# Diagonal weight matrices of a depthwise convolution built on VectorE and ScalarE instead of GpSimd

## The chip, the cores and the metric

The kernel runs on one core of a Trainium2 chip. A core has a matrix engine (TensorE, PE in the profile), VectorE (DVE), ScalarE (ACT), GpSimd (POOL) and a queue engine that issues the transfers (SyncE, SP). Each works through its own list of instructions in order, and they meet only at semaphores. The metric is the time of one execution on the device in microseconds (us); a figure for a kernel is the median of its runs.

## The reference, cut to what matters

The network has four layers on an input of 4 images of 64 x 64 positions and 96 channels. Layers 0 and 1 are state-space scans over the image in four directions, layer 2 is linear attention with a quantized feed-forward part, layer 3 a Fourier mixer with another. All is in fp32 at the interfaces. The change lies in the feed-forward part (FFN) of layer 1:

```python
def msffn(y, in_w, in_b, dw1, dw3, dw5, ln_g, ln_b, out_w, out_b):
    hcl = jax.nn.silu(y @ in_w.T + in_b)             # 192 -> 768 channels
    hc = hcl.transpose(0, 3, 1, 2)
    hc = hc + dwconv(hc, dw1) + dwconv(hc, dw3) + dwconv(hc, dw5)
    hn = layernorm(hc.transpose(0, 2, 3, 1), ln_g, ln_b)
    return hn @ out_w.T + out_b
```

`dwconv` is a depthwise convolution: each of the 768 channels has its own 1x1, 3x3 and 5x5 filter. Since all three are linear and the input is added too, they are one 5x5 filter of 25 taps for each channel.

## The kernel before, in words

`net` runs four stages one after the other: the scans of layers 0 and 1, `layer1_ffn`, `layer2` and `layer3`. Within `layer1_ffn` an image is cut into two strips of 32 rows, so there are 8 strips (n = 0 to 7), and the 768 channels into 6 tiles of 128 (t = 0 to 5). Tensors have channels on the partitions.

Once, at the start, the function loads its weights and folds the 3x3 and 1x1 filters into `taps`, a 128 x 6 x 25 tensor (lines 1244 and 1246, on VectorE). Four of the six tiles are convolved on PE (`ON_PE = (0, 2, 3, 5)`). PE can multiply by one tap for each channel if the taps stand on the diagonal of a matrix, so `diag` holds, for each of those tiles and each of the 25 taps, four 32 x 32 diagonal blocks, one for each group of 32 partitions: `eye` (the identity, stacked four times) times the tap of each partition. That makes 100 instructions of 128 x 32, on GpSimd in the kernel before (line 1249). The other two tiles (1 and 4) are convolved on VectorE, tap by tap, straight from `taps` (lines 1363 and 1365).

Then, for each strip and tile:

- `enter`: GpSimd clears a padded buffer of 36 x 68 positions (line 1289), tag `padp` with two buffers for the PE tiles and `padv` with one for the VectorE tiles. PE multiplies by the input weights in pieces of 512 positions into the PSUM tag `c` with two buffers (line 1298), and ACT applies Silu and writes the piece into the padded buffer (line 1306). A third `padp` can be cleared only when PE has finished with the first.
- `on_pe`: 25 taps times 16 small matmuls of 32 x 32 by 512 into four PSUM banks `d0` to `d3` (line 1329); then ACT copies them to `hcp` (line 1344), 16 copies for a tile.
- `on_dve`: one multiplication and 24 multiply-and-add steps over 128 x 2048 into `hcv`.
- `leave`: PE sums each finished tile over the channels into the mean (`s`, line 1375); when all six are there, the mean is subtracted (line 1410, VectorE), the squares are summed, and the strip is normalized, multiplied by the output weights (line 1455), added to the residual and stored.

The order of the instructions in each engine's list is fixed when the kernel is built. In this stage it is written by a small planner, `Plan`: each generator (`loads`, `leave`, `enter` twice, `on_pe`, `on_dve`) announces an engine and an expected time before it issues its instructions, and the planner takes the one that could start first, the earlier added one on a tie. What is issued before the planner runs, the folding of the taps and the making of the diagonals among it, announces nothing. It is ordered by the framework's own scheduler, together with the end of the stage before. In the resulting list of GpSimd stand three clearings (padp, padv, padp), then the 100 diagonals, then the clearing for the third PE tile.

Of the kernel before, what the change touches and what calls it, by code (L numbers as in the profile page):

```python
# [15 lines left out]
AF = mybir.ActivationFunctionType  # L16
# [1189 lines left out]
def layer1_ffn(k, a, x_in, y_in, x_out):  # L1206

    nc = k.nc
# [3 lines left out]
    with ExitStack() as ctx:  # L1212
# [23 lines left out]
        ON_PE = (0, 2, 3, 5)  # L1236
        taps = k.load(w, a["L1_dw5"], "taps")
        dw3 = k.load(w, a["L1_dw3"], "dw3")
        dw1 = k.load(w, a["L1_dw1"], "dw1")
        diag = k.t(w, [128, len(ON_PE), 25, 32], "diag")  # L1240
        eye = k.load(w, a["eye_blocks"], "eye")
        for t in range(NT):
            inner = taps[:, t, :].rearrange("p (y x) -> p y x", x=5)[:, 1:4, 1:4]
            nc.vector.tensor_add(inner, inner, dw3[:, t, :].rearrange("p (y x) -> p y x", x=3))
            mid = taps[:, t, 12:13]
            nc.vector.scalar_tensor_tensor(mid, mid, 1.0, dw1[:, t, :], op0=ALU.add, op1=ALU.add)
            if t in ON_PE:
                for tap in range(25):
                    nc.gpsimd.tensor_scalar_mul(diag[:, ON_PE.index(t), tap, :], eye, taps[:, t, tap : tap + 1])


        cb = k.t(w, [C, 1], "cb")
# [703 lines left out]
def net(tc, a, out):  # L1956
    with ExitStack() as ctx:
        k = Kit(tc, ctx.enter_context(tc.tile_pool(name="const", bufs=1)))
        dram = ctx.enter_context(tc.tile_pool(name="dram", bufs=1, space=DRAM))
        x1 = k.t(dram, [C, B, L], "x1")  # L1960
        x2 = k.t(dram, [C, B, L], "x2")
        x3 = k.t(dram, [C, B, L], "x3")
        y1 = k.t(dram, [DI, B, L], "y1")
        scan_layers(k, a, a["x"], x1, y1)
        layer1_ffn(k, a, x1, y1, x2)
        layer2(k, a, x2, x3)
        layer3(k, a, x3, out)
# [143 lines left out]
```

## Time and profile before

| | us |
|---|---|
| median of 3 runs | 15879.18 |
| lowest and highest run | 15832.05 and 15962.23 |
| profiled execution | 15861.73 |
| its span, first to last instruction | 15859.9 |
| the FFN of layer 1 within it | about 12750 to 14700 |

| engine | busy us | share of the span |
|---|---|---|
| PE (matmul) | 13616.6 | 86% |
| DVE | 12867.0 | 81% |
| ACT | 8291.1 | 52% |
| POOL | 9781.6 | 62% |

The shares are averages over stages that are very different. Of POOL's busy time 7186.7 us are one multiplication in the scans (line 928), and of the FFN only the start uses POOL heavily. Times in the timelines count from the span's start. In a row of groups, the figures after the shape are busy time, mean duration in ns, and the idle time of the engine just ahead of these instructions with what ended most of it. A wait in brackets names the instruction that released the waiting one.

### The profile page before, as it was taken

What the parts mean: (1) busy time and instruction counts of PE and PEld (TensorE: products, weight loads), DVE (VectorE), ACT (ScalarE), POOL (GpSimd) and SP (SyncE); (2) the same over time, 40 slices, a digit from 0 to 9 for tenths busy, and PEclk for the clock granted to TensorE, in tenths of its full rate; (3) what the DMA queues carried; (4) which work ended last, traced back from release to release, by engine and by line L of the source; (5) the groups of instructions that cost most, each with busy time, mean ns of one, the idle gap of its engine ahead of it and who ended that gap; (6) DMA issues with size and microseconds to landing.
All of it is one profiled execution on the core that took longest, in us unless ns stands there. A gap on an engine that the chain in (4) does not pass through costs nothing. (4 is left out here: it accounts for less than half of the span.)

```text
span 15859.9 us, 190275 instructions
## 1 busy us (share of the span) xinstructions
PE 13616.6 (86%) x70721; PEld 4897.8 (31%) x70721; DVE 12867.0 (81%) x9642; ACT 8291.1 (52%) x14188; POOL 9781.6 (62%) x4913
## 2 busy tenths in 40 slices
PE   7888888888888888888888888888888889998877
PEld 3222322232223222322222223222222234443344
DVE  1989798979897989799979997999899965665555
ACT  3656465556565655556655655656556522332333
POOL 0788688867886788677757775777677730000223
PEclk8888888888898888888888888888888899998888
DMA  2333433343334333433343334333433310000132
GB/s 71 110 103 121 153 108 104 120 152 106 104 122 153 106 103 120 154 109 115 113 150 118 108 118 147 111 122 116 141 118 108 115 53 18 18 11 14 46 75 70
DMA packets 662747, 1637.10 MB, mean 103 GB/s; under 512 B 102822, under 2 KB 268459, under 8 KB 658044
## 3 DMA queue, kind: packets, MB, share of 16 engines
q1 hardware_dynamic: 624956, 1549.37, 30.9%
q0 software_dynamic: 36864, 75.55, 1.6%
q8 instruction: 560, 9.18, 0.2%
q14 instruction: 367, 3.01, 0.1%
HBM read 1295.03 MB, written 329.58 MB: 102 GB/s over the span
## 5 line engine op out<-in xcount | busy, mean ns | idle before, releaser
L928 POOL TENSOR_TENSOR hc<-h,bc 128x1024 f32<-128x1024 f32 x3072 | 7186.7, 2359 | 2360.7 <-DVE h L918 1949.8
L918 DVE TENSOR_TENSOR_SCAN h<-da,state,t 128x1024 f32<-128x1024 f32 x2304 | 5271.5, 2329 | 11.5 <-ACT da L906 8.7
L939 PE MATMUL y<-hc,gather_y 128*32 128x512 f32 x12288 | 4270.8, 687 | 628.4 <-POOL hc L928 465.1
L911 DVE TENSOR_TENSOR t<-u,bc 128x1024 f32<-128x1024 f32 x3072 | 3601.2, 1218 | 895.2 <-PE u L898 780.8
L906 ACT ACTIVATE da<-dts,L_A_logs 128x1024 f32<-128x1024 f32 x3072 | 3488.0, 1147 | 726.7 <-DMA dts<-dt_dram 444.4
L898 PE MATMUL u<-dtu,spread 32*128 32x512 f32 x3072 | 1879.7, 739 | 369.4 <-DVE t L911 362.9
L962 PE MATMUL y<-L_diag,zeros 96*32 96x256 f32 x5218 | 1736.9, 463 | 0.0
L918 DVE TENSOR_TENSOR_SCAN h<-da,t 128x1024 f32<-128x1024 f32 x768 | 1711.0, 2269 | 13.1 <-ACT da L906 12.5
L939 PEld LDWEIGHTS y<-hc,gather_y 128*32 128x32 f32 x12288 | 800.1, 117 | 2404.0 <-issue 1210.4
L830 PE MATMUL m<-xs,proj 96*128 96x512 f32 (+1 forms) x2048 | 1018.3, 620 | 121.8 <-ACT dt L839 62.7
L867 ACT COPY dt<-m 96x512 f32<-96x512 f32 x512 | 297.1, 580 | 1458.9 <-PE m L862 1458.9
L898 PEld LDWEIGHTS u<-dtu,spread 32*128 32x128 f32 x3072 | 595.1, 214 | 1433.1 <-issue 1117.5
L962 PEld LDWEIGHTS y<-L_diag,zeros 96*32 96x32 f32 x5218 | 617.2, 132 | 1274.9 <-issue 1114.7
L1289 POOL MEMSET padp<- 128x2448 f32 x32 | 68.6, 2143 | 1396.7 <-PE d L1329 1375.5
L1365 DVE SCALAR_TENSOR_TENSOR hcv<-padv,taps,hcv 128x2048 f32<-128x2048 f32 x384 | 902.2, 2350 | 13.4
L1329 PE MATMUL d<-padp,diag 32*32 32x512 f32 x25600 | 885.5, 601 | 2.0 <-ACT hcp L1344 2.0
L822 POOL TENSOR_TENSOR dtu<-sp_z,dtu 96x1024 f32<-96x1024 f32 x256 | 604.4, 2361 | 384.7 <-ACT dtu L820 382.3
L862 PE MATMUL m<-sp_z,ident 96*96 96x512 f32 x1024 | 537.1, 606 | 195.6 <-ACT sp_z L856 195.6
L834 ACT ACTIVATE sp_z<-m,L_dtb 96x512 f32<-96x512 f32 x512 | 349.3, 682 | 540.4 <-PE m L830 531.6
L1329 PEld LDWEIGHTS d<-padp,diag 32*32 32x32 f32 x25600 | 483.4, 103 | 370.6 <-issue 197.7
L986 ACT COPY spare<-m 128x512 f32<-128x512 f32 x384 | 225.6, 587 | 711.0 <-PE m L983 710.8
L830 PEld LDWEIGHTS m<-xs,proj 96*128 96x128 f32 (+1 forms) x2048 | 322.4, 177 | 829.4 <-issue 325.8
(275 smaller groups left out, 15623.6 us busy)
## 6 DMA issues: line engine op xcount, KB each, us to landing
bc<-bc_dram SPq DMA_DIRECT2D x1024, 512.0 KB
dts<-dt_dram SPq DMA_DIRECT2D x768, 512.0 KB
dt_dram<-dt SPq DMA_DIRECT2D x256, 384.0 KB
y_tok<-spare SPq DMA_DIRECT2D x64, 768.0 KB
dt<-y_tok SPq DMA_DIRECT2D x128, 384.0 KB
x_tok<-y_rows SPq DMA_DIRECT2D x32, 768.0 KB
z_t<-z_rows SPq DMA_DIRECT2D x64, 384.0 KB
dx<-x_tok SPq DMA_DIRECT2D x64, 384.0 KB
```

Of the source, the lines that this page charges most:

```text
L822: rest = lambda half: nc.gpsimd.tensor_add(r[:, half], z[:, half], r[:, half])
L830: nc.tensor.matmul(ps, proj[:, src, to], xs[:, src, cols], start=src == 0, stop=src == 1)
L862: nc.tensor.matmul(ps, k.ident[:C, :C], term[:, half, cols], start=at == 0, stop=at == 2)
L898: self.nc.tensor.matmul(seg.u[:, cols], self.spread[rows, :], seg.dtu[rows, half, cols], start=True, stop=True)
L906: self.nc.scalar.activation(da, seg.dts[cb], AF.Exp, scale=seg.bt.lay.neg_a[:, seg.kd, g : g + 1])
L911: self.nc.vector.tensor_mul(gr.t, gr.seg.u, self.bc[:, 0, gr.sg, :])
L918: self.nc.vector.tensor_tensor_scan(gr.h[:, order], gr.da[:, order], gr.t[:, order], start, op0=ALU.mult, op1=ALU.add)
L928: self.nc.gpsimd.tensor_mul(gr.hc, gr.h, self.bc[:, 1, gr.sg, :])
L939: nc.tensor.matmul(seg.y[at : at + GC, :], self.gather_y, gr.hc[:, part * CH : (part + 1) * CH], start=gr.sg == 0, stop=gr.sg == NSG - 1, ...
L962: self.nc.tensor.matmul(gr.seg.y[at : at + GC, :256], self.zeros, gr.seg.bt.lay.diag.rearrange("p h t c -> p (h t c)")[:, :256], start=Fal ...
L1329: nc.tensor.matmul(pc[i][j * 32 : (j + 1) * 32, :], diag[mine, ON_PE.index(t), tap, :], pad[mine, j * 8 + dy : j * 8 + dy + 8, dx : dx + H ...
L1365: nc.vector.scalar_tensor_tensor(to, win, wt, to, op0=ALU.mult, op1=ALU.add)
```

## The change

The 100 diagonals are no longer made by GpSimd. Those of the first two PE tiles (t = 0 and 2) are made by VectorE, with the same operation; those of the other two (t = 3 and 5) by ScalarE, as an activation with the identity function and the tap as its scale, one for each partition. The values and the tensor are the same.

```diff
-            if t in ON_PE:
-                for tap in range(25):
-                    nc.gpsimd.tensor_scalar_mul(diag[:, ON_PE.index(t), tap, :], eye, taps[:, t, tap : tap + 1])
+            for tap in range(25 if t in ON_PE else 0):
+                to, one = diag[:, ON_PE.index(t), tap, :], taps[:, t, tap : tap + 1]
+
+                if t in ON_PE[:2]:
+                    nc.vector.tensor_scalar_mul(to, eye, one)
+                else:
+                    nc.scalar.activation(to, eye, AF.Identity, scale=one)
```

In the lists of the built kernel, VectorE has 50 instructions more, between the folding of the taps and its first convolution step; ScalarE has 50 more, between the last activation of the scans (line 655) and the loading of the table for Silu; GpSimd has 100 fewer, so that the clearing for the third PE tile follows the first three directly. The lists of PE and of the transfer queue are as before.

## The prediction

> **What bounds the kernel now.** I read the page first, for the stage; then the table of stretches and the waits inside that stage; then the timeline engine by engine around the operation that moves. The change touches one short place: the start of the FFN of layer 1, at 12.76 ms of a span of 15.86 ms.
>
> The page gives the chain that ended last by engine, and three groups of the stage:
>
> ```profile
> PE 12%; DVE 2%; DMA 1%; ACT 1%; issue 0%; POOL 0%; SPq 0%; ACTq 0%; POOLq 0%; DVEq 0%
> L1289 POOL MEMSET padp<- 128x2448 f32 x32 | 68.6, 2143 | 1396.7 <-PE d L1329 1375.5
> L1365 DVE SCALAR_TENSOR_TENSOR hcv<-padv,taps,hcv 128x2048 f32<-128x2048 f32 x384 | 902.2, 2350 | 13.4
> L1329 PE MATMUL d<-padp,diag 32*32 32x512 f32 x25600 | 885.5, 601 | 2.0 <-ACT hcp L1344 2.0
> ```
>
> The shares add up to some 17% of the span, because the chain is followed back only to 13.05 ms. Over that part it is PE's, so a microsecond that PE wins or loses early in the FFN should reach the end. The next view is the table of stretches (length, then busy time of PE, PE's weight loads, DVE, ACT and POOL with counts, then clock and DMA):
>
> ```profile
> 12762.90:12787.40 24.50, 18.66 (x102) 8.27 (x104) 2.72 (x16) 7.06 (x10) 24.50 (x71) 0.80 0.57 132
> 12787.40:12846.60 59.20, 37.99 (x783) 18.43 (x766) 56.45 (x25) 8.01 (x14) 59.20 (x30) 0.84 0.01 2
> ```
>
> POOL is busy for all of both, but runs 71 instructions in 24.5 us and only 30 in the next 59.2. In the second stretch PE is busy for just 38 of 59. The timelines of POOL, ACT and PE say why (start, duration, engine, line; in brackets the idle time ahead and its releaser):
>
> ```profile
> 12762.89 83.78 POOL L1249 TENSOR_SCALAR diag<-eye,taps 128x32 f32<-128x32 f32 x100
> 12846.60 2.14 POOL L1289 MEMSET padp<- 128x2448 f32 x1
> ...
> 12820.69 2.35 ACT L1344 COPY hcp<-d 32x512 f32<-32x512 f32 x4 [4.41 <-PE d L1329]
> 12823.06 0.37 ACT L1306 ACTIVATE padp<-c,in_b 128x128 f32<-128x128 f32 x1
> 12823.45 2.35 ACT L1344 COPY hcp<-d 32x512 f32<-32x512 f32 x4
> 12848.77 0.69 ACT L1306 ACTIVATE padp<-c,in_b 128x512 f32<-128x512 f32 x1 [22.98 <-POOL padp L1289]
> ...
> 12820.98 4.49 PE L1298 MATMUL c<-y,in_w 96*128 96x128 f32 x12
> 12853.16 3.72 PE L1375 MATMUL s<-hcp,avg 128*32 128x512 f32 x8 [27.70 <-ACT hcp L1344]
> ```
>
> The 100 diagonals hold POOL until 12846.6. Behind them waits the clearing of the third padp buffer; ACT stands 22.98 us for that buffer, with the evacuations of the first tile (hcp) queued behind; PE then stands 27.70 us for hcp. One chain of three waits, once in the kernel.
>
> What stands ahead of the first convolution matters for the added work:
>
> ```profile
> 12763.56 0.54 DVE L1246 SCALAR_TENSOR_TENSOR taps<-taps,dw 128x1 f32<-128x1 f32 x6
> 12785.88 1.53 DVE L1363 TENSOR_SCALAR hcv<-padv,taps 128x2048 f32<-128x2048 f32 x1 [21.78 <-ACT padv L1306]
> 12787.44 57.33 DVE L1365 SCALAR_TENSOR_TENSOR hcv<-padv,taps,hcv 128x2048 f32<-128x2048 f32 x24
> 12772.44 1.28 ACT L1306 ACT_TABLE_LOAD   x1 [21.99 <-PE c L1298]
> 12773.74 0.69 ACT L1306 ACTIVATE padp<-c,in_b 128x512 f32<-128x512 f32 x1
> 12774.48 0.30 PEld L1298 LDWEIGHTS c<-y,in_w 96*128 96x128 f32 x2 [0.95 <-ACT padp L1306]
> ```
>
> The finished taps exist at 12764.1. DVE is free from there to 12785.9, ACT only to 12772.4, and at 12774.5 PE already waits for ACT's first evacuation.
>
> **What the Trainium skill says.** "SBUF — State Buffer", section "SBUF: two separate sides": DVE and GpSimd share one pair of ports under an exclusive lock, which a DVE instruction with two SBUF inputs holds against a GpSimd operation that reads SBUF. The trace agrees: 71 diagonals in 24.5 us are 0.35 us each; once DVE's two-input steps of 2.35 us begin, 30 in 59.2 us are 1.97 us each. The DVE steps themselves keep their usual 2350 ns, so DVE wins nothing from POOL's absence. "ScalarE: Activation LUTs", section "What ACT_TABLE_LOAD costs": 186 ns + 0.833 ns per element, 93 ns more per pointer operand, and neighbours overlap by 93 ns. The trace has no activation of this form; its copies from PSUM of 96x32 are cheaper (nine in 1.03 us, line 804). "TensorE: Matmul & The Clock Gate", section "What's actually happening": an idle PE drops to half clock and needs some microseconds of work to return. The trace agrees: after the long wait eight s matmuls took 3.72 us and four c matmuls 2.61, against 2.85 and 1.98 at 12902.6 and 12905.3.
>
> **The change part by part.** PE's and SP's order of instructions are unchanged; POOL loses 100 instructions, DVE and ACT get 50 each, and no DMA moves.
>
> *POOL's 100 diagonals go.* The clearing of padp then starts when PE's first tile frees the buffer, some 0.5 us after the first hcp copy as for later tiles (12892.3 against 12891.8): 12821.2, ready at 12823.4. ACT reaches its padp step at 12823.45 + 2.35 = 12825.8, so the clearing is hidden with 2.4 us to spare. ACT's wait of 22.98 us goes entirely: **−23.0 us**. What is late next is ACT itself: PE's s matmuls follow that step by 12853.16 − 12848.77 = 4.4 us, at 12830.2, so PE still waits 30.2 − 25.5 = 4.7 us. A later tile with nearly this wait (4.43 us at 12947.2) took 3.46 us for s, and its c were back at 1.98: 0.26 + 0.63 = **−0.9 us** of cold clock. If it stays cold, 0.
>
> *DVE gets 50 diagonals* (tiles 0 and 2), behind line 1246 and ahead of its first convolution step. The nearest row is line 276 at the kernel's start, the same operation on 96x32: 17 in 2.57 us, 0.151 us each. 50 × 0.151 = 7.6 us, from 12764.1 to 12771.7. Cover: DVE's wait for padv until 12785.9; PE first reads a diagonal at 12785.4. 14 us are left, so I cost it at nothing; without the cover it would be 7.6 us. At 0.24 us each (a single one there) it would be 12 us, still hidden. No POOL work shares the port here: the third clearing ends at 12762.9.
>
> *ACT gets 50 diagonals* (tiles 3 and 5), behind the last yt of the scan stage and ahead of the table load for Silu. They can start when DVE has finished tile 3's taps, near 12764.0. By the skill's price with one pointer (the scale): 186 + 93 + 32 × 0.833 = 306 ns, less 93 of overlap, 0.213 us; 50 of them 10.7 us, to 12774.7 with the last one's tail. Table load and Silu now start at 12772.44, so they come 2.3 us later; PE's third c waits for the first Silu, so do all behind it, and with them both first convolutions: **+2.3 us**. Bounds: 0.114 us as in line 804 gives 5.7 us, hidden, +0; a second pointer for the bias gives 0.306 us, 15.4 us in all, +7.0. Below nothing is excluded: ACT has only work added here. Who waits: all c evacuations, behind them PE and DVE. Tile 3's diagonals are needed only after 12853, so the new waits of PE on ACT and DVE find their work done.
>
> Sum: −23.0 − 0.9 + 2.3 = **−21.6 us**, between −16.0 (+7.0, no clock gain) and −23.9. It must last through strip 0. DVE's second tile starts at 12916.0 after waiting 71.2 us for PE's c and ACT's padv, so it moves with PE. The padv buffer for it is cleared after DVE's first tile, near 12849.3; ACT fills it at 12886.8, then at 12865.2: 16 us spare. The y load ahead of each later strip is issued when an earlier strip is done, so it moves too. Against the profiled execution, 15861.73 us (span 15859.9), this gives 15840.1; against the median, 15879.18, it gives **15857.6 us**. The two differ by 17 us, nearly as much as the effect, and the three runs by 130; a measurement of this kernel tells about 1% (159 us) from no change.
>
> **The rivals.**
> *The gain is hidden (12%).* Another wait late in strip 0 or at its end takes the 21 us back: DVE's second tile, or the y transfer, would have to be the bound in its place. For it: PE waits for y in seven strips, 83.2 us in all. Against it: each is triggered by what moves, and the margins above are 16 us and more. Time: 15879.2.
> *ACT becomes the bound, slower than before (6%).* The place is the stretch before the Silu table load. If a diagonal costs p on ACT, the load is late by 12764.0 + 50p + 0.1 − 12772.4, and nothing is left of 23.9 us when 50p is 32.2: p = 0.64 us. At 0.8 us it ends at 12804.1, 31.7 late: 7.8 us slower, 15887.0. For it: the same operation took POOL up to 1.97 us, and a pointer scale on a tile this small is nowhere in the trace. Against it: ACT has its own ports by the same SBUF page, and the small ACT steps of the trace, up to 256 columns, stay under 0.4 us.
> *The work on ACT is free (part of the main case).* At 0.114 us: −23.9, 15855.3.
>
> **How the numbers follow.** Main case 76% (15855 to 15863), hidden 12%, ACT as the bound 6%, and 6% for what I do not see, on either side. The scatter of runs is wider than all of these. Low end: the lowest run less the gain, 15832.05 − 21.6 = 15810. High end: half-way between the middle and the highest run is 15920.7; less the gain 15899, with it hidden 15921; I take 15910 between the two. No case moves the time by 1%, so a change beyond that would come from the scatter or from the 6%: faster 2%, within 1% 95%, slower 3%.
>
> **What would show it.** Right: no wait of ACT's padp for POOL near 12825; PE's s matmuls of the first tile near 12832, after a wait of about 5 us; 50 diagonals in about 7.6 us on DVE and 10.7 on ACT, the table load near 12774.7; later strips earlier by some 21 us against the end of the scan stage. Wrong: a table load after 12780, a first convolution much after 12788, or strip 1 that starts no earlier than before. Wrong altogether: a TensorE clock in the FFN stage away from its 0.94, where 1% of PE's 1680 us is 17 us.

## The result

The changed kernel takes 15893.1 us, median of 20 runs, against 15923.51 us for the kernel before, also of 20 runs. The ratio is 0.9981 with a 95% interval of 0.9970 to 0.9992: the change makes the kernel faster by 0.19%, some 30 us (13 to 48). The forecast was a gain of 21.6 us, and 15857.6 us for the whole; the whole came out 35.5 us higher.

The changed kernel's profiled execution took 15900.73 us (span 15898.9), which is 39 us more than the profiled execution before. To see why this is no contradiction, look at SyncE's timeline for the two transfers that enclose the FFN stage: its first weight load (in_w) and the first load of layer 2 (wqkv). Here they are for the kernel before, then after:

```profile
12750.52 0.33 SPq L60 DMA_DIRECT2D in_w<-in_L_ffn_inT  x1
...
14696.59 0.24 SPq L60 DMA_DIRECT2D wqkv<-in_L_qkv  x1
```

```profile
12808.29 0.33 SPq L60 DMA_DIRECT2D in_w<-in_L_ffn_inT  x1
...
14730.89 0.24 SPq L60 DMA_DIRECT2D wqkv<-in_L_qkv  x1
```

From load to load the stage took 1946.07 us before and 1922.60 us after: **−23.5 us**. Ahead of it, in the scans, where both kernels have the same instructions, this execution came 57.8 us later; behind it layers 2 and 3 took 1163.3 and 1168.0 us. Whole executions of one kernel scatter by tens of microseconds (before: 15832.05 to 15970.63 us), so below I compare the length of this stage and places in it, counted from the issue of in_w.

The table of stretches of the changed kernel, cut at the points that answer to those shown of before (length, busy time of PE, its weight loads, DVE, ACT and POOL, clock, DMA):

```profile
12820.67:12845.42 24.75, 19.31 (x101) 8.43 (x102) 9.68 (x66) 16.38 (x54) 0.03 (x1) 0.78 0.56 128
12845.42:12904.37 58.95, 54.14 (x1051) 25.09 (x1040) 56.45 (x24) 15.39 (x26) 3.61 (x2) 0.94 0.01 2
```

In the second stretch POOL is idle but for two clearings, and PE is busy for 54.1 of 59.0 us instead of 38.0 of 59.2. DVE's busy time there is the same, 56.45 us. The timelines of POOL, ACT and PE around the place of the old wait:

```profile
12879.42 2.14 POOL L1293 MEMSET padp<- 128x2448 f32 x1 [58.72 <-PE d L1333]
...
12878.91 2.35 ACT L1348 COPY hcp<-d 32x512 f32<-32x512 f32 x4 [4.41 <-PE d L1333]
12881.28 0.37 ACT L1310 ACTIVATE padp<-c,in_b 128x128 f32<-128x128 f32 x1
12881.68 2.35 ACT L1348 COPY hcp<-d 32x512 f32<-32x512 f32 x4
12884.04 0.69 ACT L1310 ACTIVATE padp<-c,in_b 128x512 f32<-128x512 f32 x1
...
12888.42 3.72 PE L1379 MATMUL s<-hcp,avg 128*32 128x512 f32 x8 [4.73 <-ACT hcp L1348]
12892.07 2.36 PE L1302 MATMUL c<-y,in_w 96*128 96x512 f32 x4
```

The clearing now waits for PE, as it should, and is ready at 12881.6, before ACT comes to it at 12884.0. ACT no longer waits for POOL ahead of its padp step, and PE waits 4.73 us instead of 27.70. At the start of the stage, ACT and DVE:

```profile
12816.86 1.38 ACT L1253 ACTIVATE diag<-eye,taps 128x32 f32<-128x32 f32 x6 [8.65 <-DMA eye<-in_eye_blocks]
12821.22 9.43 ACT L1253 ACTIVATE diag<-eye,taps 128x32 f32<-128x32 f32 x44 [2.97 <-DVE taps L1244]
12830.67 1.28 ACT L1310 ACT_TABLE_LOAD   x1
...
12821.68 7.38 DVE L1251 TENSOR_SCALAR diag<-eye,taps 128x32 f32<-128x32 f32 x50
12844.10 1.29 DVE L1367 TENSOR_SCALAR hcv<-padv,taps 128x2048 f32<-128x2048 f32 x1 [15.04 <-ACT padv L1310]
```

DVE's 50 diagonals take 7.38 us and leave 15 us of waiting. ACT's take 9.43 us for 44, and six had been made earlier.

### The profile page after: what moved, and what is told of

Same layout as the page of the kernel before. It is cut to its first block, busy times and chain, and to the rows that moved or that the text cites. A ratio compares the mean times of both kernels' runs of the same rounds, so it can differ in the third digit from the quotient of the medians.

```text
span 15898.9 us, 190273 instructions
## 1 busy us (share of the span) xinstructions
PE 13651.7 (86%) x70721; PEld 4904.3 (31%) x70721; DVE 12866.9 (81%) x9692; ACT 8302.1 (52%) x14238; POOL 9700.2 (61%) x4813
```

## The experiments

The theory: GpSimd's list has a deadline. The third padp must be clear when ACT comes to it, about 75 us into the stage, and the 100 diagonals ahead of that clearing missed the deadline because GpSimd's operations wait for DVE's two-input steps. Rivals: every diagonal on GpSimd costs its share; the diagonals are slow there for another reason; the added work on ACT or DVE costs nothing, or costs all.

The stage in each kernel, in us from the issue of in_w; "s" is the start of PE's first sum over the first convolved tile:

| kernel | ACT waits for POOL | table load | first convolution | s | stage |
|---|---|---|---|---|---|
| before | 22.98 | 21.9 | 34.9 | 102.6 | 1946.07 |
| before, again | 23.1 | 21.5 | 34.6 | 102.4 | 1946.69 |
| after | 0 | 22.4 | 35.4 | 80.1 | 1922.60 |
| 75 on GpSimd | 0 | 21.3 | 34.3 | 79.1 | 1924.95 |
| 84 on GpSimd | 2.04 | 21.4 | 34.4 | 81.2 | 1924.92 |
| 90 on GpSimd | 16.3 | 21.6 | 34.8 | 95.9 | 1939.84 |
| 100 on DVE | 0 | 21.4 | 34.4 | 79.1 | 1921.74 |
| 100 on ACT | 0 | 32.8 | 49.2 | 93.9 | 1938.11 |
| 200 on ACT | 0 | 52.7 | 68.2 | 112.9 | 1956.23 |
| 100 on GpSimd, DVE steps left out | 0 | 20.9 | 34.8 | 79.6 | 1923.46 |
| 4 wide on GpSimd | 0 | 20.9 | 34.9 | 79.6 | 1923.88 |
| 4 wide on DVE | 0 | 21.0 | 34.0 | 78.8 | 1921.31 |

### The kernel before, again

No edit.

> The kernel before, profiled once more beside the others, for the stage's own time: from the issue of the FFN's first weight load (in_w) to the issue of the first load of the next layer (wqkv). In the first profile this was 1946.1 us, after the change 1922.6. All theories: 1946 within 1 us, with one wait of ACT's padp for POOL of 23 us; the whole time may differ by tens of us, from the scans ahead of the stage.

The stage took 1946.69 us with a wait of 23.1 us; the scans ended 88 us later than in the first profile. Two profiles of this kernel agree within 1 us in the stage, while their whole times differ by 90. Across the kernels in which ACT has no wait for POOL, those with all the work on ACT apart, the stage spreads from 1921.3 to 1925.0, each profiled once, so a difference between stages of less than 4 us is not read as an effect.

### How many may stay on GpSimd

The edit, for 75; with 90 and 84, the last tile's first 15 or 9 taps stay on GpSimd too:

```diff
-                if t in ON_PE[:2]:
-                    nc.vector.tensor_scalar_mul(to, eye, one)
-                else:
-                    nc.scalar.activation(to, eye, AF.Identity, scale=one)
+                if t in ON_PE[:3]:
+                    nc.gpsimd.tensor_scalar_mul(to, eye, one)
+                else:
+                    nc.vector.tensor_scalar_mul(to, eye, one)
```

> 75 of the 100 diagonals stay on GpSimd, 25 go to VectorE. Theory (a queue with a deadline: the clearing of the third padp only has to be ready when ACT reaches it, 75.3 us into the stage): GpSimd makes 71 at 0.35 us ahead of the convolution steps of VectorE and 4 at 1.97 us, ends some 45 us into the stage, no wait of ACT for POOL, stage 1922.2 us. Rival (each diagonal on GpSimd costs its share of the 23.5 us): 1940 us.

> 90 diagonals stay on GpSimd, 10 go to VectorE. Theory (deadline): the last ten at 1.97 us each are what is saved, GpSimd ends 19.7 us earlier than with 100, the clearing is ready 78.5 us into the stage against ACT's 75.3; ACT's wait for POOL 3.2 us, stage 1925.4. Rival (cost in proportion): wait about 20 us, stage 1944.

With 75 there was no wait and the clearing was held by PE alone, so a share of the cost for each diagonal is out: three quarters of them cost nothing that can be seen. The price was wrong all the same: GpSimd was done 57.8 us into the stage and not 45. With 90 the wait was 16.3 us, far from both 3.2 and 20. The clearing with 75, then ACT's padp step with 90:

```profile
12882.09 2.14 POOL L1293 MEMSET padp<- 128x2448 f32 x1 [12.27 <-PE d L1333]
12888.92 0.69 ACT L1310 ACTIVATE padp<-c,in_b 128x512 f32<-128x512 f32 x1 [16.32 <-POOL padp L1293]
```

Why the price failed is seen by counting the diagonals in stretches, cut where DVE's two-input steps begin and end. First the kernel before (length, POOL busy with diagonals and their number, clock, DMA), then the one with 90:

```profile
12762.89:12787.44 24.55, 24.55 (x71) 0.80 0.57 132
12787.44:12844.77 57.33, 57.33 (x25) 0.85 0.01 2
12844.77:12846.60 1.83, 1.83 (x6) 0.50 0.00 0
```

```profile
12810.05:12834.03 23.98, 23.98 (x68) 0.78 0.58 132
12834.03:12886.70 52.67, 52.67 (x23) 0.89 0.01 2
```

An instruction on a border is counted on both sides. In the kernel before, 24 or 25 diagonals fall in the 57.33 us of DVE's 24 steps, and the last five or six run at their quick pace once DVE is done. So while DVE works through its steps, one diagonal gets through for each of them, one in 57.33 / 24 = 2.39 us. My 1.97 us was a mean over this and the quick ones at the end. With 90, GpSimd had made three fewer by the time the steps began, and 22 were left for them: 22 x 2.39 = 52.6 us. The clearing started 89.3 us into the stage, only 6.8 us earlier than with 100 (96.1), not 19.7: with 100, the end of DVE's tile had in effect released GpSimd. A run to check the mended price:

> 84 diagonals on GpSimd, 16 on VectorE, after the run with 90 gave a wait of 16.3 us where 3.2 were expected. Theory, mended (while VectorE runs its two-input steps, one diagonal gets through for each step, that is one in 2.39 us; the 1.97 us used before was a mean that took in six quick diagonals after the last step): 67 are made before the steps begin 36.6 us into the stage, 17 x 2.39 = 40.6 us more, the clearing ready at 79.4 us against ACT's 75.2; ACT's wait for POOL 4.2 us, stage 1926 us. With the old price of 1.97 us the clearing would be ready at 72.2 and there would be no wait.

ACT's padp step of this run:

```profile
12951.93 0.69 ACT L1310 ACTIVATE padp<-c,in_b 128x512 f32<-128x512 f32 x1 [2.04 <-POOL padp L1293]
```

The wait was 2.04 us: there is a wait where the old price had none. It is 2.2 us under the expected one, about one DVE step: from the steps' start to the clearing's went 38.4 us, that is 16 steps and not 17. The stage was 1924.92 us; a wait of 2 us is too small to be read in it.

### Is it the DVE steps that slow GpSimd?

The diagonals stay on GpSimd as in the kernel before. The edit to DVE's convolution leaves out the 24 multiply-and-add steps of its first tile in the first strip; the one multiplication ahead of them stays:

```diff
                         if tap == 0:
                             nc.vector.tensor_scalar_mul(to, win, wt)
-                        else:
+                        elif st.n or t != ON_DVE[0]:
                             nc.vector.scalar_tensor_tensor(to, win, wt, to, op0=ALU.mult, op1=ALU.add)
```

> The diagonals on GpSimd as before; left out are the 24 multiply-and-add steps of VectorE for its first tile of the first strip, so that tile holds one tap only. Theory (GpSimd's operations wait for the two-input steps of VectorE): all 100 at 0.35 us, GpSimd ends some 47.5 us into the stage, no wait of ACT for POOL, stage 1922.2 us with no diagonal moved. Rival (the last 30 diagonals are slow for another reason, such as traffic of PE or the transfers): 1.97 us each and stage 1946.

GpSimd's timeline of this run, then the shortest, median and longest duration of a diagonal in ns, in the kernel before and in this run:

```profile
12931.33 34.37 POOL L1249 TENSOR_SCALAR diag<-eye,taps 128x32 f32<-128x32 f32 x100
12989.60 2.14 POOL L1293 MEMSET padp<- 128x2448 f32 x1 [23.89 <-PE d L1333]
...
L1249 POOL TENSOR_SCALAR diag<-eye,taps x100: 353/386/2482, 12762.9 to 12846.3; 128x32 f32<-128x32 f32 x100
L1249 POOL TENSOR_SCALAR diag<-eye,taps x100: 352/353/1407, 12931.3 to 12965.3; 128x32 f32<-128x32 f32 x100
```

All 100 take 34.37 us, 0.34 each, and the clearing waits 23.89 us for PE. The stage is 1923.46 us with no diagonal moved. So the steps of DVE were what made GpSimd late; PE and the transfers kept their work, and with it alone the diagonals run at full pace. That the steps hold GpSimd because they read two inputs is not shown by this run: the multiplication that stayed has one tensor input, and one diagonal beside it took 1.41 us, as long as that step of 1.28 us and a little more. The clearings are not held in this way: in the changed kernel the one at 12879.42 ran in the midst of DVE's steps and took its usual 2.14 us. It reads nothing, while a diagonal reads eye and the tap.

### Four wide instructions instead of 100

Against the kernel before:

```diff
             if t in ON_PE:
-                for tap in range(25):
-                    nc.gpsimd.tensor_scalar_mul(diag[:, ON_PE.index(t), tap, :], eye, taps[:, t, tap : tap + 1])
+                nc.gpsimd.tensor_mul(
+                    diag[:, ON_PE.index(t)],
+                    eye.unsqueeze(1).to_broadcast([128, 25, 32]),
+                    taps[:, t, :].unsqueeze(2).to_broadcast([128, 25, 32]),
+                )
```

and the same with `nc.vector`.

> The diagonals on GpSimd, but all 25 of a tile in one multiplication of 128x800, four instructions instead of 100. Theory: from 2.36 us for 128x1024 an estimate of 1.85 us each, 7.4 us in all, done before the convolution steps of VectorE begin; no wait, stage 1922.2 us. Rival (GpSimd is the wrong engine here whatever the number of instructions): a wait as before, 1946.

> All diagonals on VectorE, 25 in one multiplication of 128x800, four instructions. Theory: from 1.22 us for 128x1024 an estimate of 0.95 us each, 3.8 us in all, hidden; no work on ScalarE; stage 1922.2 us, that is 24 us (0.15%) under the kernel before and 0.4 us under the change. The scans ahead of the stage scatter by tens of us, so the whole times can show the sign at best: ratio 0.9985 with an interval of some 0.2% on both sides.

The two timelines:

```profile
12891.85 6.02 POOL L1248 TENSOR_TENSOR diag<-eye,taps 128x800 f32<-128x800 f32 x4 [0.79 <-DVE taps L1246]
12949.35 2.14 POOL L1293 MEMSET padp<- 128x2448 f32 x1 [51.48 <-PE d L1333]
```

```profile
12954.74 3.68 DVE L1248 TENSOR_TENSOR diag<-eye,taps 128x800 f32<-128x800 f32 x4
```

GpSimd itself, with four instructions, has finished some 17 us before DVE's steps begin, and the stage is as short as with the change. The engine was not wrong, the number of instructions was. The version on DVE has the lowest stage, 1921.31 us, though within the spread, and was timed: 15975.56 us against 16001.63 for the kernel before on the same chip, ratio 0.9983 (0.9971 to 0.9995). That beats the kernel before; whether it beats the change is not shown, since the two were timed on different chips and the ratios agree. PE's first convolution comes 1.4 us earlier than after the change (34.0 against 35.4), but the nine profiles without diagonals on ACT have it anywhere from 34.0 to 34.9, so what it saves there is some 0.5 to 1.4 us.

### What the work on DVE and ACT costs

One line for all tiles: `nc.vector.tensor_scalar_mul(to, eye, one)`, or `nc.scalar.activation(to, eye, AF.Identity, scale=one)`, the latter also twice over.

> All 100 diagonals on VectorE, none on ScalarE. Theory: 100 x 0.151 = 15.1 us, done some 28.5 us into the stage, before the first convolution reads them at about 35; hidden. Silu's table load returns to 21.9 us into the stage; stage 1922.2 us. Rival (VectorE's added work delays its own convolution and this reaches the end): 7.5 us more than after the change, 1930.

> All 100 diagonals on ScalarE, none on VectorE. Theory (ScalarE is on the path here): 50 more at 0.213 us, 10.7 us, pass in full to Silu's table load (33.1 us into the stage instead of 22.4), to the first convolution and to the end: stage 1933.3 us. Rival (the delay at the start is taken up by later waits of PE for the first strip): 1922.6.

> The 100 diagonals on ScalarE, each made twice. Theory: 150 more than after the change at 0.213 us, 32 us later, stage 1954.6: slower than the kernel before by 8.5 us, as the rival of the prediction had it for a price of 0.8 us each. Rival (delay taken up later): below 1946.

On DVE all 100 are hidden: stage 1921.74, first convolution at 34.4. On ACT nothing is hidden beyond the first few. The table load came at 32.8, 10.4 later than after the change (expected 10.7), but the first convolution 13.8 later and the stage grew by 15.5. PE's timeline of this run, then of the changed kernel, shows the rest:

```profile
12910.74 5.61 PE L1302 MATMUL c<-y,in_w 96*128 96x512 f32 x8 [8.05 <-DMA y<-y]
12928.20 14.43 PE L1302 MATMUL c<-y,in_w 96*128 96x512 f32 x28 [11.86 <-ACT padp L1310]
12942.56 5.55 PE L1333 MATMUL d<-padp,diag 32*32 32x512 f32 x160
```

```profile
12825.56 6.59 PE L1302 MATMUL c<-y,in_w 96*128 96x512 f32 x8 [8.27 <-DVE diag L1251]
12832.70 11.01 PE L1302 MATMUL c<-y,in_w 96*128 96x512 f32 x28 [0.56 <-ACT padp L1310]
12843.64 5.56 PE L1333 MATMUL d<-padp,diag 32*32 32x512 f32 x160
```

After 11.86 us of idling the same 28 matmuls take 14.43 us instead of 11.01, at a granted clock of 0.76 instead of 1.00: 3.4 us, and 10.4 + 3.4 = 13.8. The other 1.7 us of the 15.5 are within the spread of stages. With 200 on ACT the stage is 1956.23, 33.6 more than after the change (expected 32) and 9.5 to 10.2 more than before; there PE idles for 31.11 us and the 28 matmuls take 13.53 us, at a clock of 0.81. So nothing later in the strip takes up a delay of ACT at this place. The prediction's slower rival is a real mechanism, and the point from which it would lose, 32 us of work on ACT, lies between the 21 us of 100 diagonals and the 43 us of 200. What it needed was not there: at 0.21 us each, 50 are 11 us.

## Why the prediction was right or wrong

| term of the sum | predicted | measured, first profile of each |
|---|---|---|
| ACT's wait for POOL goes | −23.0 | −22.98 |
| cold clock after PE's wait | −0.9 | −0.25, within scatter |
| 50 diagonals on ACT | +2.3 | +0.45 |
| 50 diagonals on DVE | 0 | 0 |
| sum at the first convolution after the wait | −21.6 | −22.75 |
| stage | −21.6 | −23.5 |

**The step that failed** is the last one, from the sum to the forecast, and in it the base. The forecast of 15857.6 us stood on a median of three runs, 15879.18; 20 runs gave 15923.51, 44.3 us higher, about twice the effect. With that base the same sum gives 15901.9 against 15893.1 measured. Counted from the true base, 15857.6 is a fall of 65.9 us, and the measured one is 30.4. The prediction had said that its three runs spread over 130 us, and took their median all the same. The second half of the step was the judgement that a measurement of this kernel tells about 1% from no change, with 95% on a change within it. The change is within 1%, but with 20 runs of each the interval is 0.22% wide and leaves out no change: the forecast should have said "faster by a little". The sum itself lies within the interval of 13 to 48 us.

**The chain of three waits** was read rightly. The clearing is hidden, ACT itself is late next, and PE's remaining wait is 4.73 us where 4.7 was worked out.

**The cold clock** was over-priced. After a wait of 4.73 us the eight s matmuls took 3.72 us, as after 27.70, and not 3.46. The four c matmuls behind them took 2.36 us against 2.61, but that is no gain of the change: with the same wait of 4.7 us they took 2.07 with 75 on GpSimd and 3.06 with 100 on ACT, and the second profile of the kernel before has 3.04. The term cannot be told from nothing.

**ACT's diagonals** had the right price: the median is 307 ns and they follow at 9.43 / 44 = 0.214 us, which agrees with the estimates of 306 and 213 ns worked out from "ScalarE: Activation LUTs", section "What ACT_TABLE_LOAD costs", for one pointer operand. The size missed was when they start. The prediction had them wait for tile 3's taps, but the first six taps lie outside the 3x3 window that is folded in, and so wait only for eye; ACT made them 4.4 us earlier, while it was idle. The other 44 waited for the first of DVE's two folding rows, line 1244, not for the second. The table load came 0.46 us later than in the first profile, and 0.9 later than in the second one of the kernel before; the first convolution came 0.45 us later, and 0.5 to 1.4 against all nine profiles without diagonals on ACT.

So the sum came nearer to the stage than its terms deserve: 1.85 us too much for ACT's diagonals and 0.65 too much gain from the clock have opposite signs. That part is luck.

**DVE's diagonals** cost nothing: 7.38 us against 7.6, with 15.0 us of waiting behind them. The run with 100 agrees.

**The gain lasts to the end of the stage**, so the rival in which it is hidden is out: DVE's second tile started at 165.5 before and at 142.7 after, 22.8 earlier, and the next y load at 404.1 and 381.3, 22.8 earlier. ACT as the bound did not come, because the price was 0.21 us and not 0.64; the run with 200 on ACT shows that enough work there makes the stage slower than before.

**The mean price of 1.97 us** for a diagonal beside DVE's steps was not in the sum, which took the wait from the trace. It mixed two speeds, and the first experiments that used it missed by 13 us: GpSimd's end with 75, ACT's wait with 90.

What stays open: the whole times show 30 us and the stage 23.5. The difference is well within the interval, and no run tests it.

## What to carry to other kernels

A list of small instructions on GpSimd is not priced by its busy time but by what stands behind it in the same list and by what DVE does meanwhile: count instructions beside long steps of DVE, where here each step let one through. Before moving work to another engine, ask when each piece is needed; here three quarters could have stayed, and one wide instruction for each tile would have done on either engine. Where an effect is smaller than the scatter of whole runs, measure from one event to another within the trace, and split a mean where the conditions change before it is used as a price.

## What the runs showed of the hardware

- Beside DVE's two-input steps GpSimd got one operation through for each step: 24 or 25 diagonals, 0.35 us each when alone, in 24 steps of 2.39 us. DVE paid nothing in these steps: the 24 took 57.33 us with and without GpSimd's diagonals. "SBUF — State Buffer", section "SBUF: two separate sides", has the exclusive lock; the even exchange of one for one I had not expected. No GpSimd operation of another size that reads SBUF stood beside these steps here, so nothing is shown for those.
- A clearing, which reads no SBUF, ran at its usual 2.14 us in the midst of such steps.
- PE idle for 4.73 us came back as slow as after 27.7 us: eight s matmuls took 3.72 us both times. In front of the first convolution 11.86 us of idling cost 3.4 us of slow matmuls on top of the wait itself, so that a delay of 10.4 us was paid as 13.8; 31.11 us of idling cost 2.5 us, so the longer wait did not cost more.
- A multiplication of 128x800 with two broadcast inputs took 1.53 us on GpSimd and 0.975 us on DVE, against 25 x 0.344 = 8.6 us and 25 x 0.148 = 3.7 us for the same block in 25 pieces.
